# A planned order of work: when ScalarE's function tables are loaded, how far the planner looks, and how full TensorE's pauses are

## The chip, the cores and the metric

The kernel runs on one core of a Trainium2 chip. Its time is the device time of one execution in microseconds (us), here the median of three runs. A profile is taken of one further execution. The core has five engines that matter here: TensorE (PE in the profile), VectorE (DVE), ScalarE (ACT), GpSimd (POOL) and the queue of SyncE (SP), which issues all the DMA transfers.

## The reference: what is computed

Two layers act on two images of 48 x 48 positions with 768 channels, in float32. Each normalises its input by groups of channels and adds its result to it.

- Layer 0 is neighbourhood attention: a product with `w_qkv`, softmax over a window of 7 x 7 keys for each query and each of 12 heads, and a product with `w_out`.
- Layer 1 is a selective scan in two directions. `in_proj` makes x and z of 1536 channels each; x goes through a convolution of four taps and Silu (one for each direction). `x_proj` makes 80 rows, of which 48 give `delta = softplus(...)`, 16 are B and 16 are C. For each of 1536 channels and 16 states the recurrence `h = exp(delta * A) * h + delta * u * B` runs over all 2304 positions, and `y = sum over states of h * C + u * D`. The two directions' y are added, multiplied by `silu(z)` and projected back to 768 channels.

So three functions that ScalarE evaluates from tables occur: the exponential (with the logarithm in the same table set), Silu and Softplus.

## The kernel before

**Stages.** Attention of image 0 runs first and alone (some 950 us). Then comes the scan stage, to the end: the unit of work is a tile, 128 channels of one chunk of 384 positions, and there are 2 images x 2 directions x 6 chunks x 12 tiles = 288 of them. All else that is left (in_proj and x_proj of both images, attention of image 1, the output projections) is a "job" beside the scan: extra work woven in.

**A tile of the scan** (`scan`, four groups of four states each):
- the fill: `hb` is set to delta * u * B, on VectorE or GpSimd as the planner chooses for most groups (L1225);
- ScalarE writes exp(delta * A) for two states at a time into `da`, of which there are two buffers in PSUM (L1247);
- VectorE runs the recurrence in place over two states (L1258);
- GpSimd multiplies by C (L1273);
- TensorE adds the states up into `py` by transposing matmuls (L1290).

**Softplus and Silu.** For every three tiles `deltas_of` copies three products from PSUM, runs one Softplus over all three (L1162), then has the products with D (`vt`, L1170) on ScalarE and delta * u on GpSimd (L1175). In `in_proj`, `finish` runs one Silu over several tiles of x or z (L961). Each of these two functions carries, in the same closure, a load of the exponential's table set right after it (L1163, L962); the load of the function's own set is put ahead of it when the program is lowered. So a Softplus or a Silu always comes as load, function, load. Both are planned with 2600 ns for the two loads.

**The order.** All works are first collected with engine, estimated time in ns, key (the position in tiles: attention of image 0 has -56 to -16, the scan's tiles 0 to 287), buffers read and written, and marks. `Order.run` then makes a list of them for all engines by simulating: again and again it takes, of the works that are ready and whose key is at most the smallest unfinished main key plus `LOOK`, for each engine the one of lowest rank, and of these the one that can start first. The program is issued in this order; each engine executes its own works in order. The rank has two parts: the time of start plus a penalty `over`, but no less than 150 ns after the engine is free; and, for ties, the key less `early` (20 for the works that prepare a tile, 4 for those that finish one). The penalty is for works ahead of the main key that would delay a `due` work, which the exponentials L1247 are: half of the time by which the work would end more than 100 ns after `soon`, the start possible for the earliest due work.

**Pauses.** While sums of a tile are open in `py`, a planned gap of TensorE over 800 ns is partly filled with matmuls of zero effect on the sums' meaning, in columns of the bank that nobody reads (`idle`, L1491), to 0.8 of the gap less 300 ns, at 109 ns each.

Of the kernel before, what the change touches and what calls it, by code (L numbers as in the profile page):

```python
# [45 lines left out]
KB = 3  # L46
EARLY = 20
# [40 lines left out]
class Work:  # L88


    __slots__ = ("eng", "ns", "fn", "key", "job", "bufs", "waits", "then", "ready", "tail", "size", "first", "alt", "due", "opens")


class Order:
# [2 lines left out]


    SEM = 90.0
    LOOK = 2.5  # L100
    DUE = 100.0
    GAP = 800.0
    TAIL = {"PE": 120.0, "ACT": 50.0, "DVE": 45.0, "POOL": 10.0, "SP": 0.0}
# [10 lines left out]
            for p in (parts,) if isinstance(parts, int) else parts:  # L114
                yield buf, p

    def add(self, eng, ns, fn, key, r=(), w=(), job=False, size=0, after=None, early=0, alt=None, due=False, opens=None):
        x = Work()
        x.eng, x.ns, x.fn, x.key, x.job, x.size = eng, ns, fn, key, job, size
        x.then, x.ready, x.tail, x.first = [], 0.0, self.TAIL[eng], key - early  # L120

        x.alt = alt

        x.due = due

        x.opens = opens
        before, bufs = set(), {}
        for buf, p in self.cells(r):
            c = (buf, p)
            bufs[buf] = None  # L130
            if c in self.wrote:
                before.add(self.wrote[c])
            self.read.setdefault(c, []).append(x)
        for buf, p in self.cells(w):
            c = (buf, p)
            bufs[buf] = None
            if c in self.wrote:
                before.add(self.wrote[c])
            before.update(self.read.pop(c, ()))
            self.wrote[c] = x  # L140
        before.discard(x)
        if after is not None:
            before.add(after)
        x.waits = len(before)
        for y in before:
            y.then.append(x)
        x.bufs = [b for b in bufs if b.pool is not None]
        for b in x.bufs:
            b.left += 1
        self.works.append(x)  # L150
        return x

    def run(self):
        free = dict.fromkeys(self.TAIL, 0.0)
        ready = {e: [] for e in free}
        slots, dma = {}, 0.0
        mains = sorted((x.key for x in self.works if not x.job), reverse=True)
        done_keys = {}
        for x in self.works:
            if not x.waits:  # L160
                ready[x.eng].append(x)
                assert not x.alt
        out = []
        left = len(self.works)
        extra, spare = 0.0, False
        while left:
            while mains and done_keys.get(mains[-1], 0):
                done_keys[mains[-1]] -= 1
                mains.pop()
            horizon = (mains[-1] if mains else 1e9) + self.LOOK + extra  # L170
            best = None
            for e, works in ready.items():
                pick = None
                soon = min((max(free[e], x.ready) for x in works if x.due), default=1e12)
                for x in works:
                    if x.key > horizon:
                        continue
                    t, more = max(free[e], x.ready), {}
                    for b in x.bufs:
                        if not b.end:  # L180
                            had = slots.get((b.pool, b.tag), ())
                            n = more[b.tag] = more.get(b.tag, 0) + 1
                            if len(had) + n > b.bufs:
                                old = had[n - 1 - b.bufs]
                                if old.left:
                                    t = None
                                    break
                                t = max(t, old.end + self.SEM)
                    if t is None:
                        continue  # L190
                    over = 0.0
                    if mains and x.key > mains[-1] < self.last and not x.due:
                        over = max(0.0, t + x.ns - soon - self.DUE) / 2
                    rank = (max(t + over, free[e] + 150.0), x.first)
                    if pick is None or rank < pick[0]:
                        pick = rank, t, x
                if pick and (best is None or pick[1] < best[0]):
                    best = pick[1], pick[2], e
            if not best:

                extra += 1.0
                assert extra < 400, "the plan is stuck"
                continue
            extra = 0.0
            t, x, e = best
            ready[x.eng].remove(x)
            gap = t - free["PE"]
            if e == "PE" and spare and gap > self.GAP:
                y = Work()
                y.eng, y.ns, y.key, y.job, y.size = e, 0.8 * (gap - 300.0), x.key, True, 0  # L210
                y.then, y.bufs, y.due, y.fn = [], [], False, lambda y=y: self.idle(y.ns)
                out.append((free[e], y))
            if x.opens is not None:
                spare = x.opens
            if x.alt:
                ready[x.alt[0]].remove(x)
                if e != x.eng:
                    x.eng, x.ns = x.alt
            for b in x.bufs:
                if not b.end:  # L220
                    slots.setdefault((b.pool, b.tag), []).append(b)
            free[x.eng] = t + x.ns
            if x.eng == "SP":
                dma = max(dma, t + 500.0) + x.size / 290.0
                end = max(dma, t + x.ns) + 2100.0
            else:
                end = t + x.ns + x.tail
            for b in x.bufs:
                b.left -= 1
                b.end = max(b.end, end)  # L230
            for y in x.then:
                y.waits -= 1
                y.ready = max(y.ready, end + self.SEM * (y.eng != x.eng))
                if not y.waits:
                    ready[y.eng].append(y)
                    if y.alt:
                        ready[y.alt[0]].append(y)
            if not x.job:
                done_keys[x.key] = done_keys.get(x.key, 0) + 1
            out.append((t, x))  # L240
            left -= 1
        return out
# [3 lines left out]
def tile_kernel(  # L246
# [79 lines left out]
    marks = {"n": 0}  # L326
    pars = []

    def add(eng, ns, fn, key, r=(), w=(), job=False, size=0, after=None, early=0, alt=None, due=False, opens=None):

        news = [x[0] if isinstance(x, tuple) else x for x in w]

        def issue():
            for v in news:
                if v.ap is None:
                    v.ap = v.pool.tile(v.shape, F32, tag=v.tag, name=v.name, bufs=v.bufs)
            fn()

        if eng == "PE":

            ns *= 1.04 if key < 0 else 1.05
        return order.add(eng, ns, issue, key, r, w, job, size, after, early, alt, due, opens)

    def mm(n, cl):
        return n * (cl * 1.69 + 5)
# [1 line left out]
    def act(n, pointers=0):  # L347
        return 60 + 90 * pointers + n * 0.833
# [45 lines left out]
    def parameters(key):  # L394

        for i, (conv_w, conv_b, xpT, dtT, dt_b, A_log, Dp) in enumerate((fwd, bwd)):
# [15 lines left out]

            v = Buf(f"par{i}", ap=True)
            add("SP", 5000, fetch, key + i, w=[v], job=True)
            add("ACT", 800, decay, key + i + 0.5, r=[v], w=[v], job=True)
            pars.append(v)
        for j, t in enumerate(xd[0] + xd[1]):

# [8 lines left out]
    def group_norm(stats, n, key, job):  # L427
# [62 lines left out]
        for i, (eng, ns, fn, r, w) in enumerate((  # L490
# [10 lines left out]
            ("PE", 600, spread, [g, gT], [acc]),  # L501
            ("DVE", 200, last, [acc, mean], [rstd, shift]),
        )):
            add(eng, ns, fn, key + 0.01 * i, r, w, job=job)
        return shift, rstd

    def stats_of(b, key, job, tags):
# [21 lines left out]
    def attention(b, start, end, job, T):  # L529
# [228 lines left out]
        def heads(n, p, i, u, kc, ks, qs, vs, vat, mask, to, key):  # L758
# [16 lines left out]
            for j in range(2):  # L775
# [8 lines left out]
                def exponentials(j=j):  # L784
# [5 lines left out]
                add("DVE", dve(NKEY), masked, key, r=[sc[j], mask], w=[pr[j], (sm, j)], **S)  # L790
                add(
                    "ACT", act(NKEY, 1) + 90, exponentials, key, r=[pr[j], (sm, j)],
                    w=[pr[j], (sm, 2 + j)], **S,
                )

                if j or not job:
# [83 lines left out]
    def in_proj(b, i, start, end, conv=True, gate=True, nk=KB, tags=("uz",), banks=("mm",), proj=None):  # L880
# [78 lines left out]
        def finish(k0, nk, uz, dsts, key):  # L959
            def silu():  # L960
                nc.scalar.activation(uz[:, :, :, :cl], uz[:, :, :, :cl], AF.Silu)  # L961
                nc.scalar.preload_act_table_set("natural_log_exp_and_others")  # L962

            add("ACT", 2600 + act(len(dsts) * nk * cl), silu, key, r=[uz], w=[uz], job=True)
            for s, dst in enumerate(dsts):
                add(
                    "SP", 400,
# [160 lines left out]
    def deltas_of(ch, k0, x):  # L1128
# [31 lines left out]

        def softplus():
            nc.scalar.activation(dl[:, :, c], dl[:, :, c], AF.Softplus)  # L1162
            nc.scalar.preload_act_table_set("natural_log_exp_and_others")  # L1163

        add("ACT", 2600 + 120 + act(KB * cl), softplus, at + 0.05, [dl], [dl], early=EARLY)
        vts = [sb("vt", [P, CL], f"{n}_{j}") for j in range(KB)]
        for j in range(KB):
            add(
# [11 lines left out]
    def scan(ch, k, x, dlj, duj, vt):  # L1180
# [30 lines left out]
        def group(g):  # L1211
# [30 lines left out]
            def step(j):  # L1242
# [4 lines left out]
                    lambda: nc.scalar.activation(  # L1247
                        cells(da, 2)[:, j % 2, h], dl[:, jd, c], AF.Exp, scale=q["A"][:, k, i : i + 1]
                    ),
                    now + 0.06 * j - 0.06, [dlj], [(da, j % 2)], due=True,  # L1250
                )

            def two_steps(j):
# [242 lines left out]
    order.idle = idle  # L1496
    order.last = len(units) - 20
    with tc.manual_schedule():
        for _, x in order.run():
            x.fn()  # L1500


# [39 lines left out]
```

## Time and profile before

| | |
|---|---|
| median of 3 runs | 7051.39 us (7047.35 to 7055.09) |
| the profiled execution, and its span | 7056.32 us, 7054.5 us |
| TensorE, matmuls | 6334.5 us busy, 90% |
| VectorE | 6061.2 us, 86% |
| GpSimd | 5447.5 us, 77% |
| ScalarE | 4970.2 us, 70% |
| granted TensorE clock, mean | 0.975 |
| ScalarE's table loads | 341 of 1283 ns |
| fillers of TensorE's pauses | 4431, 550.4 us |

A busy TensorE is not TensorE at its peak, since matmuls overlap and their ends are modelled. GpSimd has nothing to do in the first 1040 us or so, which lowers its share and VectorE's. Groups of instructions are shown as line, engine, operation, output and inputs, count, then busy us and mean ns of one, then the idle time of the engine just before them and what ended most of it.

### The profile page before, as it was taken

The numbers are of one execution on the slowest core, as the hardware profiler recorded it, in microseconds if no ns is written. First come the engines' busy times: TensorE is split into PE (matmuls) and PEld (weight loads), VectorE is DVE, ScalarE is ACT, GpSimd is POOL, SyncE is SP. The second block draws the span as 40 slices with busy tenths as digits, with TensorE's granted clock in tenths as the row PEclk, the third lists the DMA queues.
The fourth block names the chain that finished last, engine by engine and source line by source line (L and its number), as shares of the span: only waits on it lengthen the run. The fifth ranks groups of instructions, "written<-read, shape, count | busy, mean of one in ns | idle before, by whom it ended". The sixth has DMA issues, their size and how long they took to land.

```text
span 7054.5 us, 105645 instructions
## 1 busy us (share of the span) xinstructions
PE 6334.5 (90%) x38151; PEld 4844.6 (69%) x38151; DVE 6061.2 (86%) x6217; ACT 4970.2 (70%) x10948; POOL 5447.5 (77%) x1951
## 2 busy tenths in 40 slices
PE   7999989999989998999988888888888898999888
PEld 5666656666667776676666656666678887777777
DVE  2354449999999999998898999999999999999998
ACT  1333248788887788887888778788876667777765
POOL 0000008888989999988898878999999999999997
PEclk9999989999999999999999999999999999999999
DMA  6565454444556444555444354343466676655553
GB/s 190 172 200 172 139 161 131 134 144 151 157 160 191 151 149 141 152 170 150 126 144 131 113 166 127 107 143 108 140 179 191 174 220 199 191 177 158 162 169 105
DMA packets 1337698, 1101.32 MB, mean 156 GB/s; under 512 B 136328, under 2 KB 1327416, under 8 KB 1337144
## 3 DMA queue, kind: packets, MB, share of 16 engines
q1 hardware_dynamic: 1337176, 1094.56, 52.1%
q8 instruction: 303, 4.96, 0.3%
q14 instruction: 219, 1.79, 0.1%
HBM read 881.41 MB, written 213.57 MB: 155 GB/s over the span
## 4 chain that ended last, share of the span: by engine, by line
DVE 39%; PE 19%; ACT 14%; POOL 12%; issue 9%; DMA 6%; SPq 1%; DVEq 0%; POOLq 0%; ACTq 0%
DVE hb L1258 25%; POOL hb L1273 8%; DVE hb L1225 7%; ACT da L1247 4%; PE mm_qk L382 4%; DVE uz_u L935 4%; POOL hb L1225 3%; PE py L1290 2%; PE mm_ao L382 2%; PE mm_v L382 2%; PE mm_xin L382 2%; ACT uz_u L928 1%; PE da L825 1%; ACT pr L785 1%; ACT L1163 1%
## 5 line engine op out<-in xcount | busy, mean ns | idle before, releaser
L1258 DVE TENSOR_TENSOR_SCAN hb<-da,hb 128x772 f32<-128x772 f32 x2304 | 3924.9, 1746 | 187.3 <-ACT da L1247 155.1
L1273 POOL TENSOR_TENSOR hb<-hb,bc 128x1536 f32<-128x1536 f32 x1152 | 3653.7, 3186 | 381.0 <-DVE hb L1258 338.3
L1247 ACT ACTIVATE da<-dlt,A 128x384 f32<-128x384 f32 x4608 | 2677.2, 584 | 915.2 <-DVE hb L1258 845.8
L1290 PE MATMUL py<-ident,hb 128*128 128x128 f32 x13824 | 1754.3, 279 | 264.3 <-POOL hb L1273 255.2
L1290 PEld LDWEIGHTS py<-ident,hb 128*128 128x128 f32 x13824 | 1570.9, 143 | 523.5 <-POOL hb L1273 413.6
L1225 POOL TENSOR_TENSOR hb<-u,bc 128x1544 f32<-128x1544 f32 x495 | 1584.6, 3203 | 22.6 <-PE py L1290 14.9
L1225 DVE TENSOR_TENSOR hb<-du,bc 128x1544 f32<-128x1544 f32 x657 | 1141.4, 1743 | 34.3 <-ACT du L1202 24.8
L1175 POOL TENSOR_TENSOR u<-dlt,u 128x384 f32<-128x384 f32 x288 | 263.8, 918 | 532.7 <-DMA bc<-xdf 412.6
L382 PE MATMUL mm_xin<-xc,w_x 128*128 128x390 f32 x1656 | 593.3, 504 | 25.3 <-DVE uz_u L935 16.2
L382 PE MATMUL mm_z<-xc,w_z 128*128 128x384 f32 x1728 | 608.1, 492 | 7.8 <-ACT dlt L1157 4.9
L382 PE MATMUL mm_out<-stage_y,w_o 128*128 128x192 f32 x3168 | 560.7, 332 | 18.1 <-ACT dlt L1157 6.4
L1491 PE MATMUL py<-ident 128*128 128x128 f32 x4431 | 550.4, 277 | 0.0
L382 PEld LDWEIGHTS mm_out<-stage_y,w_o 128*128 128x128 f32 x3168 | 522.0, 194 | 29.3 <-ACT dlt L1157 10.6
L1491 PEld LDWEIGHTS py<-ident 128*128 128x128 f32 x4431 | 503.3, 143 | 28.9 <-issue 26.0
L901 POOL MEMSET xc<- 128x18 f32 x4 | 0.5, 116 | 637.2 <-DVE sm L779 637.2
L382 PEld LDWEIGHTS mm_xin<-xc,w_x 128*128 128x128 f32 x1656 | 311.3, 195 | 238.3 <-issue 36.7
L935 DVE SCALAR_TENSOR_TENSOR uz_u<-mm_xin,conv_w,uz_u 128x384 f32<-128x384 f32 x792 | 428.3, 607 | 52.0 <-ACT uz_u L928 49.4
L382 PE MATMUL mm_qk<-xc_xn,w_qk 128*128 128x384 f32 x1296 | 459.1, 500 | 14.7 <-DMA w_qk<-in_w_qkv 3.1
L382 PEld LDWEIGHTS mm_z<-xc,w_z 128*128 128x128 f32 x1728 | 314.3, 192 | 194.4 <-issue 8.9
L382 PEld LDWEIGHTS mm_qk<-xc_xn,w_qk 128*128 128x128 f32 x1296 | 240.2, 194 | 173.8 <-issue 19.5
L785 ACT ACTIVATE pr<-pr,sm 128x308 f32<-128x308 f32 x432 | 234.5, 544 | 127.5 <-DVE sm L779 127.2
L1306 PE MATMUL py<-ident,vt 128*128 128x128 f32 x864 | 156.3, 292 | 146.3 <-ACT yt L1316 145.9
(163 smaller groups left out, 6780.9 us busy)
## 6 DMA issues: line engine op xcount, KB each, us to landing
w_o<-in_w_opT SPq DMA_DIRECT2D x264, 384.0 KB
bc<-xdf SPq DMA_DIRECT2D x96, 768.0 KB
bc<-xdb SPq DMA_DIRECT2D x96, 768.0 KB
w_qk<-in_w_qkv SPq DMA_DIRECT2D x144, 384.0 KB
w_x<-in_w_inT SPq DMA_DIRECT2D x144, 384.0 KB
w_z<-in_w_inT SPq DMA_DIRECT2D x144, 384.0 KB
w_ao<-in_w_out SPq DMA_DIRECT2D x72, 384.0 KB
u<-uf SPq DMA_DIRECT2D x48, 576.0 KB
```

The source lines that it names most:

```text
L382: nc.tensor.matmul(acc[:m, o0 : o0 + cl], wb[:, wi, wo : wo + m], xb[:, xi, xo : xo + cl], start=c == 0, stop=c == n - 1,)
L785: nc.scalar.activation(pr[j].ap, pr[j].ap, AF.Exp, bias=sm[:, j : j + 1], scale=-1.0, accum_out=sm[:, 2 + j : 3 + j],)
L825: nc.tensor.transpose(bank(pt, 512 - P)[:nk, k * P : (k + 1) * P], pr[j][:, c0 : c0 + nk], ident,)
L935: nc.vector.scalar_tensor_tensor(u, px[:, at[j] : at[j] + cl], q["conv_w"][:, k, j : j + 1], u, ALU.mult, ALU.add,)
L1175: lambda j=j: nc.gpsimd.tensor_mul(u[:, j, h], dl[:, j, c], u[:, j, h]), at + 0.06 + 0.25 * j,
L1225: on.tensor_mul(cells(hb, SG), by.unsqueeze(1).to_broadcast([P, SG, W]), bc[g].ap)
L1247: lambda: nc.scalar.activation(cells(da, 2)[:, j % 2, h], dl[:, jd, c], AF.Exp, scale=q["A"][:, k, i : i + 1]),
L1258: lambda: nc.vector.tensor_tensor_scan(flip(hb[at2]), flip(da[:, : 2 * W]), flip(hb[at2]), 0.0, ALU.mult, ALU.add),
L1273: lambda: nc.gpsimd.tensor_mul(cells(hb, SG)[:, :, h], cells(hb, SG)[:, :, h], bc[NSG + g][:, :, c]),
L1290: nc.tensor.matmul(py[:tp, t * P : (t + 1) * P], cells(hb, SG)[:, j, h][:, tb[t]], ident, start=False, stop=g == NSG - 1 and j == SG - 1 a ...
L1306: nc.tensor.matmul(py[:tp, t * P : (t + 1) * P], vt[:, tb[t]], ident, start=t == 0, stop=False, is_transpose=True, skip_group_check=True,)
L1491: nc.tensor.matmul(marks["py"][:, CL : CL + P], ident, ident, start=False, stop=False, is_transpose=True, skip_group_check=True,)
```

## The change

It has three parts.

1. **Tables.** A work can name the table set it needs: "exp" for the exponentials, the decay's exponential and the group norm's logarithm and exponential, "silu" and "softplus". `Order.run` keeps the set that ScalarE would have at that point and adds 1294 ns to a work whose set differs, once it is chosen. Silu and Softplus lose their 2600 ns and the load behind them; instead the loop that issues the works puts a load of the exponential's set directly ahead of an exponential that follows another function. While a set other than the exponential's is in, a Silu or Softplus has its second rank part lowered by 20.
2. **Look.** `LOOK` goes from 2.5 to 3.5 tiles.
3. **Pauses.** A gap is filled to 0.9 instead of 0.8 of its length less 300 ns.

```diff
@@ class Order
-    LOOK = 2.5
+    LOOK = 3.5
@@ Order.add (and tile_kernel's add, which passes it on)
+        x.table = table
@@ Order.run
-        extra, spare = 0.0, False
+        extra, spare, table = 0.0, False, "exp"
...
-                    rank = (max(t + over, free[e] + 150.0), x.first)
+
+                    own = x.table not in (None, "exp") and table != "exp"
+                    rank = (max(t + over, free[e] + 150.0), x.first - 20 * own)
...
-                y.eng, y.ns, y.key, y.job, y.size = e, 0.8 * (gap - 300.0), x.key, True, 0
+                y.eng, y.ns, y.key, y.job, y.size = e, 0.9 * (gap - 300.0), x.key, True, 0
+                y.table = None
...
+            if x.table and x.table != table:
+                x.ns += 1294.0
+                table = x.table
@@ in_proj, finish
                 nc.scalar.activation(uz[:, :, :, :cl], uz[:, :, :, :cl], AF.Silu)
-                nc.scalar.preload_act_table_set("natural_log_exp_and_others")
-
-            add("ACT", 2600 + act(len(dsts) * nk * cl), silu, key, r=[uz], w=[uz], job=True)
+
+            add(
+                "ACT", act(len(dsts) * nk * cl), silu, key, r=[uz], w=[uz], job=True, table="silu",
+            )
@@ deltas_of
             nc.scalar.activation(dl[:, :, c], dl[:, :, c], AF.Softplus)
-            nc.scalar.preload_act_table_set("natural_log_exp_and_others")
-
-        add("ACT", 2600 + 120 + act(KB * cl), softplus, at + 0.05, [dl], [dl], early=EARLY)
+
+        add("ACT", 120 + act(KB * cl), softplus, at + 0.05, [dl], [dl], early=EARLY, table="softplus")
@@ scan, step (and in the same way decay, root and the softmax's exponentials)
-                    now + 0.06 * j - 0.06, [dlj], [(da, j % 2)], due=True,
+                    now + 0.06 * j - 0.06, [dlj], [(da, j % 2)], due=True, table="exp",
@@ the loop that issues the works
     with tc.manual_schedule():
+        table = "exp"
         for _, x in order.run():
+            if x.table == "exp" != table:
+                nc.scalar.preload_act_table_set("natural_log_exp_and_others")
+            table = x.table or table
             x.fn()
```

`act(n)` is 60 + 0.833 n ns.

More of the change, by code (lines that the diff above doesn't have):

```diff
@@ L88 @@
 class Work:
-    __slots__ = ("eng", "ns", "fn", "key", "job", "bufs", "waits", "then", "ready", "tail", "size", "first", "alt", "due", "opens")
+    __slots__ = ("eng", "ns", "fn", "key", "job", "bufs", "waits", "then", "ready", "tail", "size", "first", "alt", "due", "opens", "table")
 class Order:
     SEM = 90.0
-    LOOK = 2.5
+    LOOK = 3.5
     DUE = 100.0
@@ L115, in cells, with add @@
                 yield buf, p
-    def add(self, eng, ns, fn, key, r=(), w=(), job=False, size=0, after=None, early=0, alt=None, due=False, opens=None):
+    def add(self, eng, ns, fn, key, r=(), w=(), job=False, size=0, after=None, early=0, alt=None, due=False, opens=None, table=None):
         x = Work()
@@ L327, in tile_kernel, with add @@
     pars = []
-    def add(eng, ns, fn, key, r=(), w=(), job=False, size=0, after=None, early=0, alt=None, due=False, opens=None):
+    def add(eng, ns, fn, key, r=(), w=(), job=False, size=0, after=None, early=0, alt=None, due=False, opens=None, table=None):
         news = [x[0] if isinstance(x, tuple) else x for x in w]
@@ L341, in add @@
             ns *= 1.04 if key < 0 else 1.05
-        return order.add(eng, ns, issue, key, r, w, job, size, after, early, alt, due, opens)
+        return order.add(eng, ns, issue, key, r, w, job, size, after, early, alt, due, opens, table)
     def mm(n, cl):
@@ L414, in parameters @@
             add("SP", 5000, fetch, key + i, w=[v], job=True)
-            add("ACT", 800, decay, key + i + 0.5, r=[v], w=[v], job=True)
+            add("ACT", 800, decay, key + i + 0.5, r=[v], w=[v], job=True, table="exp")
             pars.append(v)
@@ L503, in group_norm @@
         )):
-            add(eng, ns, fn, key + 0.01 * i, r, w, job=job)
+            add(eng, ns, fn, key + 0.01 * i, r, w, job=job, table="exp" if fn is root else None)
         return shift, rstd
@@ L792, in heads @@
                     "ACT", act(NKEY, 1) + 90, exponentials, key, r=[pr[j], (sm, j)],
-                    w=[pr[j], (sm, 2 + j)], **S,
+                    w=[pr[j], (sm, 2 + j)], table="exp", **S,
                 )
```

## Prediction

> **What bounds the kernel now.** I read the busy table by stages first. Its columns are the stretch, its length, then busy time (and count) of the TensorE matmuls, weight loads, VectorE, ScalarE and GpSimd, then clock and DMA:
>
> ```profile
> 0.00:1050.00 1050.00, 959.77 (x5007) 632.69 (x5008) 420.08 (x1504) 306.93 (x835) 1.60 (x11) 0.97 0.57 171
> 1050.00:4250.00 3200.00, 2894.44 (x17442) 2140.30 (x17440) 2955.46 (x2737) 2588.93 (x5832) 2809.35 (x1001) 0.98 0.49 149
> 4250.00:5250.00 1000.00, 870.00 (x5269) 677.90 (x5270) 968.80 (x785) 793.74 (x1590) 940.69 (x335) 0.98 0.43 131
> 5250.00:7054.00 1804.00, 1610.25 (x10437) 1393.75 (x10435) 1716.88 (x1193) 1280.58 (x2694) 1695.84 (x605) 0.97 0.60 174
> ```
>
> The first 1050 us (attention of image 0) belong to TensorE. In the other 6004 us VectorE works 5641 us and GpSimd about 5446; ScalarE only 4663. VectorE is idle 245 of 3200 us (7.6%) up to 4250 and 118 of 2804 us (4.2%) after it; GpSimd 391 (12.2%) and 168 (6.0%). So the scan stage has a floor some per cent away, and only idle time on these two is to be won. Next the groups, costliest first:
>
> ```profile
> L1258 DVE TENSOR_TENSOR_SCAN hb<-da,hb 128x772 f32<-128x772 f32 x2304 | 3924.9, 1746 | 187.3 <-ACT da L1247 155.1
> L1273 POOL TENSOR_TENSOR hb<-hb,bc 128x1536 f32<-128x1536 f32 x1152 | 3653.7, 3186 | 381.0 <-DVE hb L1258 338.3
> L1225 POOL TENSOR_TENSOR hb<-u,bc 128x1544 f32<-128x1544 f32 x495 | 1584.6, 3203 | 22.6 <-PE py L1290 14.9
> L1225 DVE TENSOR_TENSOR hb<-du,bc 128x1544 f32<-128x1544 f32 x657 | 1141.4, 1743 | 34.3 <-ACT du L1202 24.8
> ```
>
> The fill (L1225) runs on either engine, 1743 ns against 3203 ns, so GpSimd's time is worth 1743/3203 = 0.544 of VectorE's. If x us of idle go on VectorE and y on GpSimd, the end moves by (x + 0.544 y)/1.544. I use this throughout; it assumes that the planner rebalances.
>
> Then the waits of the scan stage, VectorE's and GpSimd's (total us, times, longest):
>
> ```profile
> DVE hb L1258 <- ACT da L1247: 155.1, 116, 6.3
> POOL hb L1273 <- DVE hb L1258: 338.3, 199, 13.4
> POOL u L1175 <- ACT vt L1170: 94.8, 43, 8.9
> ```
>
> ScalarE's exponentials keep VectorE waiting 155 us; GpSimd's long wait is VectorE's lateness passed on. Last, ScalarE's table loads, by line (count, busy, mean ns), and one place in time order (start, length):
>
> ```profile
> L1162 ACT ACT_TABLE_LOAD x96 | 123.2, 1283 | 1.5
> L1163 ACT ACT_TABLE_LOAD x96 | 123.2, 1283 | 1.6
> ...
> L961 ACT ACT_TABLE_LOAD x74 | 94.9, 1283 | 1.3
> L962 ACT ACT_TABLE_LOAD x74 | 94.9, 1283 | 1.3
> ```
>
> ```profile
> 1201.55 1.28 ACT L1163 ACT_TABLE_LOAD   x1
> 1202.84 0.48 ACT L955 COPY uz_z<-mm_z 128x384 f32<-128x384 f32 x1
> 1203.34 1.28 ACT L961 ACT_TABLE_LOAD   x1
> ```
>
> The load at 1201.55 is wasted: a Copy and then a Silu follow. But that is rare: in ScalarE's order, five Silu follow a Silu, two a Softplus, and two Softplus follow a Silu, with no exponential between. All others have exponentials on both sides.
>
> **What the Trainium skill says.** "ScalarE: Activation LUTs", section What ACT_TABLE_LOAD costs, gives 1283 ns for a load plus a drain of about 1380 ns. The trace agrees on 1283 and shows no such drain: 1201.55 to 1202.84 is 1.29 us from start to start. I use 1.29. The section Table sets of the same page says that cheap functions such as copy and identity are in every set; so a Copy between Silu and the next exponential needs no load. No run here shows it yet. "TensorE: Matmul & The Clock Gate", HAM oscillation, says that TensorE gaps above about 3.4 us bring the clock down; the trace has 0.975 on average, with fillers (L1491, 4431) already in the gaps.
>
> **The change part by part.**
> (1) Loads dropped by placing alone. A Silu after a Silu saves two, the mixed pairs one: 5 x 2 + 4 = 14 of 340. Eleven lie in the start-up (977 to 1050 us), where six Silu come before any exponential. There three loads stand on the chain that ended last:
>
> ```profile
> 1002.09 1.28 ACT L962
> ...
> 1024.59 1.28 ACT L961
> ...
> 1027.38 1.28 ACT L962
> ```
>
> They lead to the small projection, its store and the first fetch of the scan's factors, so I count them fully: -3.9 us. If something else is late by then, 0.
>
> (2) Loads dropped by "like together". The bonus of 20 acts only between works that tie in the first part of the rank (within 150 ns of ScalarE's free time). A Silu or Softplus ahead of the main key carries the penalty `over` whenever an exponential is due, and after a block of several us one nearly always is. I take 20 loads; none and 80 (about half of the 164 blocks of the scan stage giving up one load) are the ends. 23 loads with the three left of (1) are 30 us of ScalarE. VectorE's exposed share: 155 us of waiting against 326 x 1.283 + 74 x about 2.1 + 96 x 1.17 = 686 us of blocks, 0.23. So x = 7 us, 4.5 us at the end. Ends: 0 and 17.
>
> (3) Exponential load moved. It no longer stands right behind Softplus but ahead of the next exponential. The skip products (L1170), which rank 20 tiles early, now run before it, and GpSimd's product (L1175) waiting for them starts up to 1.28 us sooner: 43 waits x 1.28 = 55 us at most. I take half, y = 28, which is 0.544 x 28/1.544 = 10 us. The load costs the same ScalarE time later; if a Copy waiting for TensorE stands between, a load that used to hide in that wait is exposed, up to as much: ends -20 to +10.
>
> (4) Penalties. The planned cost of Silu falls from 2600 + 60 + 2304 x 0.833 = 4579 to 1979 ns, Softplus from 3740 to 1140; the load is charged only after the choice, and the exponential's load to the exponential. With over = (t + ns - soon - 100)/2, such a work beats an exponential due later by more than (ns - 100)/3: Silu 1493 ns before, 626 now; Softplus 1213, 347. So blocks start with exponentials nearer, and these come 0.87 us later each: 164 x 0.87 = 142 us of lateness. The work that hides it is the second da buffer (one scan, 1.75 us) and fills and convolution taps on VectorE. I take 0.1 exposed: 14/1.544 = +9 us. Cover gone: +92. It could also be 0, since Softplus whose key has come due carries no penalty in either version.
>
> (5) LOOK 3.5. A tile lasts about 6004/288 = 20.8 us, so jobs, weight fetches and stage loads are eligible 20.8 us earlier where buffers are free: more fillers to choose from on VectorE and TensorE, nothing new to do. SP issues sooner and buffers (two PSUM banks `mm`, two `uz`) fill with later work. If it brought 1050 to 4250 halfway to the idle shares after 4250, x = 1.7% and y = 3.1% of 3200, 55 and 99 us: 71 us. I take a fifth, -14; the trace gives no value, and the reverse is open to the same size, since the whole order is replanned.
>
> (6) Pauses 0.9. 4431 x 0.9/0.8 = 4985 fillers, +554 x 124 ns (550.4/4431) = 69 us of TensorE in gaps. Cover: gaps beyond the fill. For a gap of 2 us, 0.8 x 1.7 us planned at 109 ns takes 1.55 us at 124, and now 1.74: 0.26 us remain. Taken at 0; a higher clock could give 10 us (2.5% of TensorE's chain outside attention, about 6% of the span), a late add-up (L1290, 2% of the chain) cost 10.
>
> Sum: -3.9 - 4.5 - 10 + 9 - 14 = -23. The profiled execution took 7056.3 (span 7054.5 and 1.8 around it): 7033. It lies 4.9 above the median 7051.4, so 7028.
>
> **Rivals.**
> A, a little faster as summed, 7028; own range 6995 to 7037.
> B, the longer look fills the gaps up to 4250 as in (5)'s bound: -71 and -5 net of the rest, about 6975. For it: 7.6% idle there against 4.2%. Against: the scans wait for ScalarE and single DMAs too, not for lack of fillers alone.
> C, within 0.2% (7037 to 7065): ScalarE is at 78% in the scan stage and its loads hide under VectorE and GpSimd.
> D, slower: (4) decides. Place: `da` L1247 behind Softplus and Silu, scans queued behind it on VectorE, then GpSimd. With 0.75 of 142 us exposed, 69 us at the end, less 4 + 4.5 + 10: +50, about 7100. It turns from gain to loss where more than 32 x 1.544/142 = 35% of the lateness is exposed. The mean exposure now is 23%, but the buffered scan is used up already by a block of 3.7 us, so the next 0.87 us may be dearer.
>
> **How the numbers follow.** Chances: A 0.42, B 0.12, C 0.12, D 0.34. Faster by over 0.2% (14 us, about what a measurement tells from no change) is A and B less the little of A above it: 0.53; same 0.12; slower 0.35. For 8 in 10: one in ten lies below 6968 (most of B) and one in ten above 7118 (the upper third of D, towards cover gone).
>
> **What would show it.** Table loads: about 307; above 325 refutes (2). The three chain loads gone by 1031 us. Softplus followed by L1170 and only then a load (3). The wait of the scans for `da`: below 150 us confirms A, above 200 us D. VectorE idle before 4250: 190 instead of 245 for B. Fillers near 4985 (6); fewer means the gaps themselves shrank. The prediction is wrong if the replanned order collides elsewhere, for example GpSimd waiting for a fetch of bc.

## The result, and the profile after

The changed kernel takes 7083.34 us (median of 4 runs, 7076.70 to 7087.52) against 7053.24 us for the kernel before, measured beside it (median of 4, 7047.35 to 7064.39): a ratio of 1.0037, with a 95% interval of 1.0026 to 1.0049. It is slower by some 0.4%, where the prediction had 0.3% faster as the likeliest. The time lies inside the stated range, on its other side.

The profiled execution took 7081.73 us, with a span of 7079.9 us. Lines of `kernel.py` lie eight or more further down than before: L1255 is the exponential (L1247 before), L1266 the scan (L1258), L1281 the product with C (L1273), L1233 the fill (L1225), L1171 Softplus (L1162), L1178 and L1183 the two products behind it (L1170, L1175), L1510 the exponential's table load, which now stands in the loop that issues.

Busy time by stretch, columns as before (matmuls, weight loads, VectorE, ScalarE, GpSimd, clock, DMA):

```profile
0.00:1050.00 1050.00, 971.76 (x5058) 635.42 (x5059) 428.30 (x1509) 310.10 (x847) 13.56 (x18) 0.98 0.58 175
1050.00:4250.00 3200.00, 2914.51 (x17726) 2162.49 (x17725) 2944.18 (x2730) 2558.75 (x5784) 2761.79 (x983) 0.98 0.49 148
4250.00:5250.00 1000.00, 885.21 (x5525) 694.84 (x5524) 965.42 (x777) 790.31 (x1583) 947.99 (x337) 0.99 0.42 126
5250.00:7079.00 1829.00, 1648.78 (x10806) 1429.87 (x10804) 1738.20 (x1208) 1294.59 (x2723) 1714.60 (x612) 0.98 0.61 174
```

From 1050 us on VectorE is busy 5648 of 6029 us and GpSimd 5424: idle 381 and 605 us, where it was 363 and 558. By the prediction's own exchange rate that is (18 + 0.544 x 47)/1.544 = 28 us, the whole loss. The groups of these two engines have kept their durations (mean ns after the busy us), and their counts within four fills:

```profile
L1266 DVE TENSOR_TENSOR_SCAN hb<-da,hb 128x772 f32<-128x772 f32 x2304 | 3924.7, 1747 | 210.8 <-ACT da L1255 182.0
L1281 POOL TENSOR_TENSOR hb<-hb,bc 128x1536 f32<-128x1536 f32 x1152 | 3656.5, 3190 | 391.9 <-DVE hb L1266 347.4
L1233 POOL TENSOR_TENSOR hb<-u,bc 128x1544 f32<-128x1544 f32 x491 | 1573.2, 3206 | 12.4 <-PE py L1298 9.0
L1233 DVE TENSOR_TENSOR hb<-du,bc 128x1544 f32<-128x1544 f32 x661 | 1148.1, 1743 | 47.6 <-ACT du L1210 32.2
```

So nothing got slower; two engines wait more. The waits of the scan stage (total us, times, longest) say for what: ScalarE, by 27 us on VectorE and by 58 us on GpSimd.

```profile
DVE hb L1266 <- ACT da L1255: 182.0, 158, 6.8
...
POOL hb L1281 <- DVE hb L1266: 347.4, 214, 7.7
POOL u L1183 <- ACT vt L1178: 152.6, 59, 7.5
```

The table loads by line (count, busy, mean ns); with the single load at the program's start there are 329, instead of 341:

```profile
L1510 ACT ACT_TABLE_LOAD x163 | 209.1, 1283 | 2.7
L1171 ACT ACT_TABLE_LOAD x96 | 123.2, 1283 | 1.5
L969 ACT ACT_TABLE_LOAD x69 | 88.5, 1283 | 1.2
```

And ScalarE in time order around one Softplus (start, length), where the load has moved as described, behind two Copies:

```profile
1044.42 1.16 ACT L1171 ACTIVATE dlt<-dlt 128x1152 f32<-128x1152 f32 x1
1045.49 0.18 ACT L1239 COPY bc<-zero 128x8 f32<-128x8 f32 x1
1045.58 0.47 ACT L963 COPY uz_z<-mm_z 128x384 f32<-128x384 f32 x1
1046.07 1.28 ACT L1510 ACT_TABLE_LOAD   x1
```

Where along the way is the time lost? The start of every 576th scan, by the traces:

| scan | before | after | difference |
|---|---|---|---|
| 1st | 1056.7 | 1042.9 | -13.8 |
| 577th | 2583.8 | 2591.0 | +7.2 |
| 1153rd | 4180.7 | 4226.6 | +45.9 |
| 1729th | 5657.6 | 5672.1 | +14.5 |
| last | 7016.1 | 7039.3 | +23.1 |

The start-up gains 14 us, and the scan stage loses 37 between its first and its last scan: more than that in the first half, of which the second gives some back.

### The profile page after: what moved, and what is told of

It is laid out like the page before. It is cut to its first block, busy times and chain, and to the rows that moved or that the text cites. A ratio compares the mean times of both kernels' runs of the same rounds, so it can differ in the third digit from the quotient of the medians.

```text
span 7079.9 us, 107532 instructions
## 1 busy us (share of the span) xinstructions
PE 6420.3 (91%) x39108; PEld 4922.6 (70%) x39108; DVE 6076.1 (86%) x6221; ACT 4953.7 (70%) x10936; POOL 5437.9 (77%) x1947
## 4 chain that ended last, share of the span: by engine, by line
DVE 38%; PE 20%; ACT 17%; POOL 11%; issue 9%; DMA 5%; SPq 0%; DVEq 0%; POOLq 0%; ACTq 0%
DVE hb L1266 25%; POOL hb L1281 7%; DVE hb L1233 7%; ACT da L1255 5%; PE mm_qk L390 4%; DVE uz_u L943 3%; POOL hb L1233 3%; PE mm_v L390 2%; PE py L1298 2%; PE mm_ao L390 2%; PE mm_xin L390 2%; ACT L1510 1%; ACT pr L793 1%; PE da L833 1%; DMA bc<-xdb 1%
## 5 line engine op out<-in xcount | busy, mean ns | idle before, releaser
L1266 DVE TENSOR_TENSOR_SCAN hb<-da,hb 128x772 f32<-128x772 f32 x2304 | 3924.7, 1747 | 210.8 <-ACT da L1255 182.0
L1281 POOL TENSOR_TENSOR hb<-hb,bc 128x1536 f32<-128x1536 f32 x1152 | 3656.5, 3190 | 391.9 <-DVE hb L1266 347.4
L1255 ACT ACTIVATE da<-dlt,A 128x384 f32<-128x384 f32 x4608 | 2674.5, 584 | 928.8 <-DVE hb L1266 850.3
L1233 POOL TENSOR_TENSOR hb<-u,bc 128x1544 f32<-128x1544 f32 x491 | 1573.2, 3206 | 12.4 <-PE py L1298 9.0
L1233 DVE TENSOR_TENSOR hb<-du,bc 128x1544 f32<-128x1544 f32 x661 | 1148.1, 1743 | 47.6 <-ACT du L1210 32.2
L1183 POOL TENSOR_TENSOR u<-dlt,u 128x384 f32<-128x384 f32 x288 | 264.8, 920 | 568.5 <-ACT dlt L1171 409.3
L1499 PE MATMUL py<-ident 128*128 128x128 f32 x5388 | 652.7, 275 | 0.0
L1499 PEld LDWEIGHTS py<-ident 128*128 128x128 f32 x5388 | 603.7, 141 | 33.0 <-issue 28.8
L1160 PE MATMUL mm_dl<-dt,dtw 49*128 49x384 f32 x576 | 250.1, 538 | 52.2 <-DMA dtw<-dtT 15.7
```

The lines of the kernel that those rows point to most:

```text
L1160: lambda j=j, acc=acc: nc.tensor.matmul(acc[:, c], w[:, j * P : (j + 1) * P], dt[:, c], start=True, stop=True),
L1183: lambda j=j: nc.gpsimd.tensor_mul(u[:, j, h], dl[:, j, c], u[:, j, h]), at + 0.06 + 0.25 * j,
L1233: on.tensor_mul(cells(hb, SG), by.unsqueeze(1).to_broadcast([P, SG, W]), bc[g].ap)
L1255: lambda: nc.scalar.activation(cells(da, 2)[:, j % 2, h], dl[:, jd, c], AF.Exp, scale=q["A"][:, k, i : i + 1]),
L1266: lambda: nc.vector.tensor_tensor_scan(flip(hb[at2]), flip(da[:, : 2 * W]), flip(hb[at2]), 0.0, ALU.mult, ALU.add),
L1281: lambda: nc.gpsimd.tensor_mul(cells(hb, SG)[:, :, h], cells(hb, SG)[:, :, h], bc[NSG + g][:, :, c]),
```

## Experiments

The theory after the result is the prediction's step 4, as rival D had it: Silu and Softplus, cheaper by 2600 ns in the penalty, start with the next exponential nearer, and ScalarE is late for the scans. The rivals: the longer look, the fuller pauses, the load that moved, and chance, since every change of an estimate gives another order of thousands of works. Each run's ratio is against the kernel before as measured beside it, whose median then lay between 7053.7 and 7055.7 us.

**The parts alone.** First the tables' part, with look 2.5 and pauses 0.8:

```diff
 (the kernel after)
-    LOOK = 3.5
+    LOOK = 2.5
...
-                y.eng, y.ns, y.key, y.job, y.size = e, 0.9 * (gap - 300.0), x.key, True, 0
+                y.eng, y.ns, y.key, y.job, y.size = e, 0.8 * (gap - 300.0), x.key, True, 0
```

> The tables' part alone: look 2.5 and pauses 0.8 as before. If the lowered penalty (the theory of step 4) makes the loss, this is slower than before by about 30 to 45 us (7083 to 7098), since the start-up still gains some 10 us, and the scans wait for da about 180 us instead of 155. If the longer look makes the loss, it is 10 to 20 us faster than before (7033 to 7043) by the start-up's dropped loads and the earlier skip products. If the pauses make it, the same.

Measured: 7073.57 us, ratio 1.0023 (1.0014 to 1.0033). The wait for `da` is 201.9 us. Slower, as the penalty theory has it, though by 18 us rather than 30 to 45, and with a wait above the 180 expected.

The look alone:

```diff
 (the kernel before)
-    LOOK = 2.5
+    LOOK = 3.5
```

> The kernel before with LOOK 3.5 and nothing else. The prediction's step 5 expects 14 us faster (7039). If the look makes the loss: 20 to 50 us slower (7073 to 7103), with VectorE's idle time before 4250 up. The penalty theory expects it within 15 us of before.

Measured: 7062.29 us, ratio 1.0011 (1.0003 to 1.0019). The first scan starts 17.0 us earlier than before, at 1039.7, so the start-up's gain in the changed kernel is mostly the look's; it is gone by the 1153rd scan (+17.4 us) and the last stands at +5.5.

The pauses alone:

```diff
 (the kernel before)
-                y.eng, y.ns, y.key, y.job, y.size = e, 0.8 * (gap - 300.0), x.key, True, 0
+                y.eng, y.ns, y.key, y.job, y.size = e, 0.9 * (gap - 300.0), x.key, True, 0
```

> The kernel before with pauses of 0.9 and nothing else; the order of all real work stays as it is, so no replanning is mixed in. Prediction's step 6: within 5 us of before, about 4985 fillers. If the fillers push real matmuls back: 10 to 40 us slower, with GpSimd and ScalarE waiting longer for py. If the clock matters: up to 10 us faster and a mean clock above 0.975.

Measured: 7051.87 us, ratio 0.9996 (0.9988 to 1.0004), mean clock 0.976 in the profiled execution against 0.975. This is the cleanest of the runs: ScalarE's and VectorE's instructions come in the same order as before, at every place. The fillers' group:

```profile
L1491 PE MATMUL py<-ident 128*128 128x128 f32 x5007 | 616.3, 277 | 0.0
```

There are 576 more of them and 66 us more of TensorE's time, and the end doesn't move. The pauses are out. Tables, look and pauses alone cost 18, 7 and -4 us, 21 together; all at once they cost 30.

**The penalty put back.** In the changed kernel the penalty alone reckons Silu and Softplus with 2600 ns more; planned times, loads, look and pauses stay:

```diff
 (the kernel after)
-                        over = max(0.0, t + x.ns - soon - self.DUE) / 2
+                        over = max(0.0, t + x.ns + 2600.0 * (x.table in ("silu", "softplus")) - soon - self.DUE) / 2
```

> The kernel after with the penalty of Silu and Softplus reckoned as before (2600 ns are added in the penalty alone, not in the planned time). Penalty theory: the loss goes, 7030 to 7050, and the scans' wait for da falls to about 155 us or less. Look or pauses as the cause: unchanged at 7075 to 7090.

Measured: 7029.12 us, ratio 0.9962 (0.9949 to 0.9975): 54 us better than the changed kernel, and better than before. The waits have shrunk on both engines:

```profile
POOL hb L1281 <- DVE hb L1266: 290.4, 160, 14.0
...
DVE hb L1266 <- ACT da L1255: 148.4, 113, 6.6
...
POOL u L1183 <- ACT vt L1178: 99.5, 46, 8.3
```

Then the same with look 2.5 and pauses 0.8:

> Tables with the penalty reckoned as before, look 2.5, pauses 0.8. Prediction's steps 1 to 3 without 4, 5 and 6: 18 us faster than before, 7037. If the longer look is needed for the gain of the kernel with the penalty restored: the same as before, 7045 to 7060; if the look costs: about 7020.

Measured: 7015.81 us, ratio 0.9945 (0.9932 to 0.9957), 58 us under the tables' part without the penalty (7073.57), and below all that was expected; the shuffle below tells how much of that is the luck of one order.

**The converse, in the old kernel.** Loads and planned times as before, only the penalty without the 2600 ns:

```diff
 (the kernel before)
-                        over = max(0.0, t + x.ns - soon - self.DUE) / 2
+                        over = max(0.0, t + x.ns - 2600.0 * (e == "ACT" and x.ns > 2600.0) - soon - self.DUE) / 2
```

> The kernel before, loads placed and planned as before (341 of them), look 2.5 and pauses 0.8; only the penalty of Silu and Softplus is reckoned without the 2600 ns. Penalty theory: this alone makes it slower, 7075 to 7110, with Softplus blocks starting when the next exponential is about 1 us away instead of 2.1. If the gain of the last experiment came from a lucky order: anywhere within 20 us of before. If the moved load is what hurts in the kernel after (a load exposed ahead of the exponential): no change, 7045 to 7065.

Measured: 7123.80 us, ratio 1.0095 (1.0080 to 1.0109). One term of the planner's rank, with the same 341 loads, costs 69 us, more than the 20 to 55 or so that were expected. So neither the moved load nor the grouping is needed for the loss.

**Softplus or Silu.** The penalty put back for one of the two in the kernel after (`x.table in ("softplus",)`, `x.table in ("silu",)`), and lowered for one of the two in the kernel before (`and not x.job` added for Softplus, `and x.job` for Silu):

> The kernel after with the 2600 ns put back into the penalty of Softplus alone. In the trace of after only Softplus blocks start earlier against the next exponential (1.08 us before it could start, 2.11 before the change); Silu blocks do not (2.12 against 2.20). If that reading is right, this wins most of the 54 us: 7025 to 7045. If Silu matters as much, about half: 7050 to 7060.

> The kernel after with the 2600 ns put back into the penalty of Silu alone. If Softplus carries the loss: still slower than before, 7065 to 7100. If both matter: about 7055.

> The kernel before with the penalty reckoned without the 2600 ns for Softplus alone. If Softplus carries the loss: most of the 69 us that both together cost, 7095 to 7130. If both matter: 7080 to 7095.

> The kernel before with the penalty reckoned without the 2600 ns for Silu alone. If Softplus carries the loss: within 15 us of before, 7040 to 7070. If both matter: 7080 to 7095.

Measured, in this order: 7039.74 (ratio 0.9975, 0.9964 to 0.9985), 7083.57 (1.0039, 1.0026 to 1.0051), 7125.63 (1.0101, 1.0087 to 1.0115), 7055.07 us (1.0002, 0.9993 to 1.0010). Softplus carries the loss in both kernels, 44 of 54 us in the new one, where the rest is within the scatter told below, and all of it in the old one; Silu carries none that can be told. Lowering Silu's penalty in the old kernel leaves ScalarE's order as it was for its first 6969 of 10,948 instructions.

One Softplus shows how the cover is lost. In the kernel before, ScalarE's row and then VectorE's:

```profile
1135.99 1.28 ACT L1162 ACT_TABLE_LOAD   x1
1137.28 1.17 ACT L1162 ACTIVATE dlt<-dlt 128x1152 f32<-128x1152 f32 x1
1138.47 1.28 ACT L1163 ACT_TABLE_LOAD   x1
```

```profile
1133.91 3.22 DVE L935 SCALAR_TENSOR_TENSOR uz_u<-mm_xin,conv_w,uz_u 128x384 f32<-128x384 f32 x6
1137.05 3.41 DVE L1258 TENSOR_TENSOR_SCAN hb<-da,hb 128x772 f32<-128x772 f32 x2
1140.38 1.74 DVE L1225 TENSOR_TENSOR hb<-du,bc 128x1544 f32<-128x1544 f32 x1
```

The Softplus is placed where VectorE is on six convolution taps with two scans' exponentials in stock; VectorE doesn't pause. In the old kernel with Softplus' penalty lowered, at the same time:

```profile
1136.04 1.28 ACT L1162 ACT_TABLE_LOAD   x1
1137.33 1.16 ACT L1162 ACTIVATE dlt<-dlt 128x1152 f32<-128x1152 f32 x1
1138.50 1.28 ACT L1163 ACT_TABLE_LOAD   x1
1139.79 0.48 ACT L1202 COPY du<-u 128x386 f32<-128x386 f32 x1
```

```profile
1132.92 5.11 DVE L1258 TENSOR_TENSOR_SCAN hb<-da,hb 128x772 f32<-128x772 f32 x3
1140.31 1.77 DVE L1225 TENSOR_TENSOR hb<-du,bc 128x1544 f32<-128x1544 f32 x1 [2.27 <-ACT du L1202]
```

Here VectorE is in the middle of scans and runs dry: 2.27 us of idle time, ended by a Copy that stood behind the Softplus and its load. So not only exponentials come late: VectorE's wait for this Copy (`du`) in the whole scan stage rises from 24.8 to 60.0 us in this kernel, and that for `da` from 155.1 to 183.6.

Over all of them, worked out from the instructions' times in the traces: for each Softplus after 1060 us (94 or 95 in a trace), the block starts 1.29 us ahead of the function, and the next exponential could start when the scan two places back ended, since `da` has two buffers. Columns: how long after the block's start it could start, how late it then started (means, us, good to about 0.05); the time in the 9 us from each block's start in which VectorE, and GpSimd, ran nothing (sums, us); the median time.

| kernel | could start | late by | VectorE idle | GpSimd idle | time |
|---|---|---|---|---|---|
| before | 2.11 | 2.74 | 81 | 87 | 7053 |
| before, Softplus' penalty lowered | 0.88 | 3.73 | 123 | 146 | 7126 |
| after | 1.08 | 3.37 | 94 | 136 | 7083 |
| after, penalty put back | 2.13 | 3.00 | 95 | 88 | 7029 |
| tables alone | 1.16 | 3.62 | 122 | 155 | 7074 |
| tables alone, penalty put back | 2.21 | 2.66 | 76 | 66 | 7016 |

The loss goes with GpSimd's column more than with VectorE's: putting the penalty back in the kernel after wins 54 us, and VectorE's column stays. For Silu the first column is 2.20 before and 2.12 after, and the stretches behind it have not become idler (VectorE 84 us before, 85 after; GpSimd 134, 125).

**How much is chance.** Three orders shuffled by an estimate without meaning: the changed kernel with a load planned at 1290 instead of 1294 ns, the tables' part with the penalty put back likewise, and the kernel before with 2590 ns for Softplus' loads instead of 2600.

> A change without meaning: the kernel after with a table load planned at 1290 instead of 1294 ns, to see how far the time moves when the order is merely shuffled. Penalty theory: it stays slower than before, 7070 to 7095. If single orders scatter by 50 us, it can lie anywhere from 7030 to 7130.

> The kernel of 7015.8 us (tables, penalty restored, look 2.5, pauses 0.8) with a load planned at 1290 instead of 1294 ns, a change without meaning. Penalty theory: 7005 to 7035, faster than before. If its gain was a lucky order: 7040 to 7080.

> The kernel before with Softplus planned at 2590 instead of 2600 ns for its loads, a change without meaning: 7040 to 7070 if the time of before is typical of its kind of order; below 7030 if before was an unlucky order, and then the gain of the tables' part is smaller than it looked.

Measured: 7094.32 (ratio 1.0053, 1.0041 to 1.0066), 7041.03 (0.9985, 0.9976 to 0.9993), 7069.46 us (1.0017, 1.0011 to 1.0024). So they lie 11, 25 and 14 us above the orders they come from. One order is a draw with a scatter of that size, and only differences seen in several orders count. By what was expected of it, the second says that some of the 7015.81 us was a lucky order, though a part of the gain on the kernel before stays. The penalty's difference is: 54, 58, 69 and 44 us in four pairs, 72 with Softplus alone in the old kernel. The longer look's (7 us) is not above the scatter.

**Other doses.** With look 2.5 and pauses 0.8, 1300 and 5200 ns in the penalty instead of 2600, and the first with a load planned at 1290 ns:

> Tables with look 2.5 and pauses 0.8, and 1300 ns put back into the penalty of Silu and Softplus instead of 2600. With 0 ns this kernel took 7073.6, with 2600 ns 7015.8. Penalty theory: in between, 7030 to 7060, with Softplus blocks starting about 1.6 us ahead of the next possible exponential. If only shuffling is at work: no relation, 7010 to 7100.

> The kernel with half the penalty restored (1300 ns, look 2.5, pauses 0.8) and a load planned at 1290 instead of 1294 ns. If the half dose's 7078.8 was the scatter of one order: 7030 to 7060. If half of it doesn't help at all, a threshold: 7070 to 7095.

> The same with 5200 ns put back. If ever later blocks keep paying: 6990 to 7010. If what comes behind Softplus (the products on GpSimd) then gets late: 7020 to 7060, with GpSimd waiting longer for vt. Shuffling: no relation.

Measured: 7078.84 (ratio 1.0030, 1.0019 to 1.0042), 7076.37 (1.0032, 1.0021 to 1.0044), 7040.64 us (0.9978, 0.9969 to 0.9987). The half dose was to lie in between, and doesn't: both orders, 2 us apart, are as slow as with none. More than 2600 brings nothing beyond the scatter, nor does GpSimd wait longer for `vt` (81.6 us). The half dose also limits what the table above explains: its Softplus blocks leave 1.95 and 1.99 us until the next exponential and make it 2.69 and 2.73 us late, nearly the values of before, and VectorE idles 84 and 81 us behind them. What is still high is GpSimd's idle time there, 109 and 110 us. In the waits of the first:

```profile
DVE hb L1266 <- ACT da L1255: 180.6, 139, 6.7
...
POOL u L1183 <- ACT vt L1178: 123.8, 50, 10.8
```

against the tables' part with 2600 ns:

```profile
DVE hb L1266 <- ACT da L1255: 163.5, 126, 7.7
...
POOL u L1183 <- ACT vt L1178: 75.9, 36, 10.8
```

GpSimd's idle time behind Softplus divides all the traces: 62 to 94 us in those with 2600 or 5200 ns in Softplus' penalty, 109 to 155 in those with less.

Why `vt` comes late can be read from the same traces. The skip product that makes `vt` does not need Softplus, so ScalarE can run it on either side. GpSimd's product waits for both: it reads what Softplus writes, and overwrites the u that the skip product reads. An earlier Softplus stands ahead of the first of its three skip products more often, and GpSimd's first product then follows that skip product more closely. For the Softplus after 1060 us: how many stand ahead, the mean time from the skip product's end to the start of GpSimd's product, and GpSimd's waits for that skip product (sum):

| kernel | Softplus ahead | us between | waits, us | time |
|---|---|---|---|---|
| before | 24 of 95 | 11.2 | 22 | 7053 |
| before, Softplus' penalty lowered | 44 of 95 | 4.8 | 55 | 7126 |
| after | 58 of 94 | 4.0 | 67 | 7083 |
| after, penalty put back | 38 of 94 | 8.2 | 18 | 7029 |
| tables alone | 47 of 95 | 5.3 | 71 | 7074 |
| tables alone, half the penalty | 37 of 95 | 7.0 | 52 | 7079 |
| tables alone, penalty put back | 29 of 95 | 10.1 | 24 | 7016 |

The middle column divides all the traces too: 8.2 to 11.5 us with Softplus' penalty whole or doubled, 7.1 or less below (the waits don't quite: 18 to 45 and 37 to 83 us). So it goes with the half dose, which the timing against the exponentials does not. It is a reading of traces: no run held Softplus back behind its skip product and left the rest alone.

Taken together, the kernels with the tables' part took 7016 to 7041 us in the five orders with Softplus' penalty whole or doubled, and 7074 to 7094 in the six with less. Those with the old loads took 7052 to 7069 with it whole and 7124 and 7126 without. Neither pair of ranges overlaps, and the gaps, 33 and 54 us, are above the scatter: that the term costs time is shown. And with the penalty whole, every kernel with the tables' part (two of the five have the longer look, one has twice the penalty) is faster than every one with the old loads, by 25 us on average.

## Why the prediction was wrong

**Step 4 failed, by its size.** It named the edit that decides and gave its price from both sides, 0 to 92 us, and then took 9, with 0.1 of the lateness exposed. Measured are 44 to 58 us in kernels with the tables' part, 69 and 72 in the old one. Its first half held for Softplus: the blocks start about 1 us nearer (2.11 to 1.08), where the thresholds gave 0.87. Three things after that were off.

- It spread the effect over Silu and Softplus alike, 164 blocks; only the 96 of Softplus moved and cost.
- The share exposed was judged by the mean over all blocks (0.23) and then lowered. But the cover that was named, fills and taps on VectorE, was not there by itself: in the place shown, at 1136 us, the old penalty had put Softplus where VectorE was on taps, and without it the block fell among scans.
- GpSimd was left out, but for lateness passed on. From the kernel after to the one with the penalty put back, VectorE's idle time after 1050 us falls from 381 to 352 us and GpSimd's from 605 to 508 (busy 5615 and 5459 of 5967 us); by the prediction's exchange rate that is 19 and 34 us, 53 together for the 54 measured. In the old kernel with Softplus lowered, VectorE's rises by 60 us and GpSimd's by 71 (busy 5650 and 5444 of 6073 us), which is 39 and 25, 64 for the 72 measured. In the changed kernel GpSimd's wait for `vt` is 53 us of it (152.6 to 99.5) and its wait for the scans, which passes VectorE's lateness on, 57 (347.4 to 290.4); other waits grew by some 14.

How late the exponentials come does not price the loss by itself: with the penalty put back they are later than before (3.00 against 2.74 us) in a faster kernel, and at half the penalty no later (2.69) in a slower one.

**Rival D** had the direction, the edit and the first engine. That its 7100 us is near 7083 is in part luck: it counted Silu's blocks too and put the price on the scans' wait for `da`, whose mark, above 200 us, was not reached (182.0), since part of the loss went through GpSimd's wait for `vt`. (Two figures of the prediction don't follow from its own steps: in rival B the rest of the sum is -9, not -5, and the upper end of step 2 is 16, not 17. Neither changes anything here.)

**Step 1 was right.** The six Silu of the start-up share one load, and the three loads are gone from the chain. The first scan of the tables' part alone starts 4.8 us earlier (1051.9), for 3.9 predicted.

**Step 2 was refuted** by its own mark: 329 loads, above 325. In ScalarE's order five Silu follow a Silu, all in the start-up, and two mixed pairs have no exponential between: 5 x 2 + 2 = 12 loads, fewer than the 14 expected from placing alone. The bonus joined nothing.

**Step 3** had the order right; its 10 us are not shown by themselves. GpSimd's wait for `vt`, which was to fall, rose from 94.8 to 152.6 us with the low penalty, and is 75.9 to 116.8 in the three orders with 2600 ns back for both functions. Steps 1 to 3 together were 18 us; the two orders with the tables' part and the penalty put back are 39 and 15 us faster than before. The forecast lies between them, but they differ from each other by more than it.

**Step 5** took -14 for the look: it measured +7 alone, not distinguishable from a shuffle. That a replanned order could go either way, by the same size, was said. Such draws came out at 2 to 25 us, as large as the whole forecast gain of 23, so the single figure that the sum gave could not have told much about one order.

**Step 6 was right**: 5007 fillers for 4985, nothing at the end, nothing from the clock. In the full change, with another order of work, there are 5388.

Still open: whether GpSimd's lost slack behind the skip products is the cause of the part of the loss that goes through it, since no run changed it alone; and why Silu's place hardly answers to its own penalty.

The best version run is the tables' part with the penalty put back, look 2.5 and pauses 0.8: 7015.81 us (0.9945), and 7041.03 us (0.9985) when shuffled. Both beat the kernel before and the changed one; 0.15 to 0.55% over the kernel before is what can be claimed.

## What to carry to other kernels

When a cost moves from one work to another in a planner, look for every other place that reads the old number: here 2600 ns of loads were also what kept a long function away from exponentials that were due, and taking them out of that comparison cost more than the loads saved. Average cover is no guide for a work whose place was chosen for its cover. Shuffle the order by a meaningless amount before believing a gain or a loss of some tenths of a per cent.

## What the runs showed of the hardware

Copies ran between a Softplus and the exponential's load (1045.49 and 1045.58 above) without a load of their own, as the Trainium skill, "ScalarE: Activation LUTs", section Table sets, says of cheap functions; the trace of before couldn't show it. That 576 more fillers, 66 us of TensorE's time, cost nothing and moved the mean clock by only 0.001 was within the prediction's bounds. Every table load took 1283 ns, 341 before and 329 after. In the trace of before 340 of them started within 0.02 us of the end of ScalarE's instruction ahead, and 320 had the next instruction starting at most 1.31 us after their own start; the others were followed by longer gaps, which were not looked into.
